# Layer 1 of a two-layer attention kernel: the two halves of the softmax sums merged by VectorE, the ones product in four column tiles of 256 columns

## The chip, the cores and the metric

The kernel runs on one core of a Trainium2 chip. The time is device microseconds of one execution; medians of several executions are given. In what follows, TensorE is PE in the profile, VectorE is DVE, ScalarE is ACT, PEld is TensorE's loading of weights, and the queue of SyncE, from which the transfers here are issued, is SPq.

## The reference, cut to what matters

Two attention layers over eight images of 64 channels and 64 x 64 positions, so 4096 queries and keys per image. Layer 0 has 8 channels in its scores; layer 1 normalises by groups, has 64 channels in its scores, and adds a projection.

```python
# layer 0
s = einsum('bci,bcj->bij', f, g); beta = softmax(s, axis=2)
o = einsum('bcj,bij->bci', hh, beta); x = x + o
# layer 1
attn = softmax(einsum('bqc,bkc->bqk', q, k) * scale, axis=-1)
out = einsum('bqk,bkc->bqc', attn, v)        # then a projection, + x
```

Each softmax needs the sum of the exponentials over all keys, one number per query. The change is about that sum in layer 1.

## The kernel before

A stage is one image in one layer. It has four chunks of 2 x 512 queries (h is the half of the queries), and a chunk has 16 steps of two key tiles (p = 0 and 1). In each step TensorE makes scores (s), ScalarE takes the exponential (e), TensorE weighs the values with it (acc, in PSUM), and VectorE adds e to a running sum (esum), 128 x 2048 elements. The stages follow in the order 0, 1, then alternating: layer 1 of image b-2 alternates with layer 0 of image b. During a layer-1 stage the next layer-0 image is prepared, at fixed steps.

When a chunk ends, this happens (cut; in order of the source):

```python
def finish(self, acc, esum, c, index):
    raw = work.tile([P, CW], F32, tag="raw", bufs=3, ...)
    self.total(raw, acc)              # copies the accumulator out of PSUM
    ...
    def sums(spare):                  # five steps later in layer 1
        for p in range(2):
            for h in range(2):        # ones product: sum over the 128 partitions
                matmul(z[ts(2*h+p, 32), :], ones, esum[:, p, h, :],
                       start=True, stop=True, tile_position=(0, 32*(2*h+p)))
        zs = work.tile([P, CW], F32, tag="zs", ...)
        nc.scalar.copy(zs, z)
        for h in range(2):
            for p in range(2):        # rows dealt over partitions by transfers
                row = 32 * (2*h + p)
                nc.sync.dma_start(zt[ts(h, C), p, :], zs[row : row+1, :])

    def reciprocals():
        nc.vector.tensor_add(zh, zt[:, 0, :], zt[:, 1, :])
        nc.vector.reciprocal(rt, zh)
        ...                           # to DRAM and back, spread over partitions
    def result():
        nc.vector.tensor_mul(raw, raw, r)
        self.residual(raw, c)

# layer 1
def total(self, raw, acc):
    nc.vector.tensor_copy(raw, acc[0])
    nc.vector.tensor_add(raw, acc[1], raw)

# layer 0, preparation of an image: steps of the stage in which it is done
return [(20, begin, True), (25, lambda: self.project(1), True)] + [...]
```

The accumulator of layer 1 has two banks, and those are all that its pool has; the next chunk's weighing can't start before `total` has copied them (in the trace of before, TensorE waits 0.88 us for that copy at 1258 us). VectorE works its queue in order: in that trace exponentials that ScalarE finished at 1223.59 and 1227.08 us are summed only from 1230.41 on, after VectorE had stood 7.61 us for the transfer of the sums. And `project` of the preparation issues 16 transfers of f and g rows from the same queue as the transfers of the sums.

## Time and profile before

| | before |
|---|---|
| time, median of 3 | 3190.0 us (3187.82 to 3190.19) |
| span of the profiled run | 3188.0 us |
| TensorE busy | 3116.8 us, 98% |
| VectorE busy | 2450.2 us, 77% |
| ScalarE busy | 2083.4 us, 65% |
| mean granted clock of TensorE | 0.996 |

The share of busy time says what an engine does over the whole span; the chain of waits (part 4 of the page) says whose work the end depended on. The lines of both are in the prediction.

### The profile page before, as it was taken

The numbers are of one execution on the slowest core, as the hardware profiler recorded it, in microseconds if no ns is written. First come the engines' busy times: TensorE is split into PE (matmuls) and PEld (weight loads), VectorE is DVE, ScalarE is ACT, GpSimd is POOL, SyncE is SP. The second block draws the span as 40 slices with busy tenths as digits, with TensorE's granted clock in tenths as the row PEclk, the third lists the DMA queues.
The fourth block names the chain that finished last, engine by engine and source line by source line (L and its number), as shares of the span: only waits on it lengthen the run. The fifth ranks groups of instructions, "written<-read, shape, count | busy, mean of one in ns | idle before, by whom it ended". The sixth has DMA issues, their size and how long they took to land.

```text
span 3188.0 us, 58576 instructions
## 1 busy us (share of the span) xinstructions
PE 3116.8 (98%) x25525; PEld 1106.0 (35%) x25525; DVE 2450.2 (77%) x1588; ACT 2083.4 (65%) x2257; POOL 16.7 (1%) x41
## 2 busy tenths in 40 slices
PE   7999999999999999999999999999999999999997
PEld 2333334333333334333333333333333333334432
DVE  6899766887678876788767887679866798666665
ACT  6787655776557765577655875558855587555554
POOL 2000000000000000000000000000000000000000
PEclk9999999999999999999999999999999999999999
DMA  3100010100101001010010100101001000000000
GB/s 69 34 8 17 11 34 8 28 21 8 35 8 28 21 8 34 8 28 21 8 34 8 31 19 7 38 5 35 18 5 41 2 21 18 5 21 15 9 14 15
DMA packets 66408, 63.54 MB, mean 20 GB/s; under 512 B 39408, under 2 KB 39488, under 8 KB 66144
## 3 DMA queue, kind: packets, MB, share of 16 engines
q1 hardware_dynamic: 65024, 59.56, 7.9%
q8 instruction: 202, 3.31, 0.4%
q14 instruction: 62, 0.51, 0.1%
q0 software_dynamic: 800, 0.15, 0.0%
q10 hardware_dynamic: 320, 0.01, 0.0%
HBM read 25.33 MB, written 8.65 MB: 11 GB/s over the span
## 4 chain that ended last, share of the span: by engine, by line
PE 87%; ACT 5%; DVE 4%; issue 2%; DMA 1%; SPq 0%; DVEq 0%; ACTq 0%
PE acc_l L122 51%; PE s_l L122 31%; ACT e_l L623 5%; DVE esum_l L595 3%; PE z_l L122 2%; PE qk_l L122 1%; PE v_l L122 1%; DMA r_l<-recips 0%; PE fg_l L122 0%; SPq L306 0%; DMA zt_l<-zs_l 0%; DVE split_l L371 0%; DVE vt_l L276 0%; DMA recips<-stash 0%; DMA x<-in_x_dram 0%
## 5 line engine op out<-in xcount | busy, mean ns | idle before, releaser
L623 ACT ACTIVATE e_l<-s_l 128x1024 f32<-128x1024 f32 x2048 | 1967.5, 1025 | 1062.0 <-PE s_l L122 1062.0
L595 DVE TENSOR_TENSOR esum_l<-esum_l,e_l 128x2048 f32<-128x2048 f32 x896 | 2050.6, 2289 | 390.1 <-ACT e_l L623 347.3
L122 PE MATMUL acc_l<-e_l,vt_l 64*64 64x512 f32 (+1 forms) x12288 | 1959.5, 595 | 6.7 <-DVE raw_l L524 5.9
L122 PE MATMUL s_l<-kq_l 64*64 64x512 f32 x8192 | 992.2, 589 | 1.5 <-DVE ve_l L443 1.5
L122 PEld LDWEIGHTS acc_l<-e_l,vt_l 64*64 64x64 f32 (+1 forms) x12288 | 594.2, 134 | 1067.2 <-issue 963.9
L122 PEld LDWEIGHTS s_l<-kq_l 64*64 64x64 f32 x8192 | 343.7, 133 | 543.0 <-issue 534.7
L122 PE MATMUL s_l<-fg_l 32*128 32x512 f32 x2048 | 272.0, 472 | 23.6 <-ACT e_l L623 15.5
L122 PEld LDWEIGHTS s_l<-fg_l 32*128 32x128 f32 x2048 | 108.0, 182 | 345.0 <-ACT e_l L623 213.2
L595 DVE TENSOR_TENSOR esum_l<-e_l,e_l 128x2048 f32<-128x2048 f32 x64 | 146.2, 2285 | 78.4 <-ACT e_l L623 78.4
L320 DVE TENSOR_TENSOR raw_l<-raw_l,r_l 128x512 f32<-128x512 f32 x64 | 44.0, 688 | 84.7 <-DMA r_l<-recips 84.7
L310 DVE TENSOR_TENSOR zh_l<-zt_l 128x8 f32<-128x8 f32 x64 | 10.5, 164 | 106.4 <-DMA zt_l<-zs_l 106.4
L122 PE MATMUL z_l<-esum_l,ones 128*32 128x512 f32 x512 | 68.4, 606 | 1.5 <-DVE vt_l L276 1.3
L524 DVE COPY raw_l<-acc_l 128x512 f32<-128x512 f32 x32 | 22.1, 690 | 41.5 <-PE acc_l L122 41.5
L302 ACT COPY zs_l<-z_l 128x512 f32<-128x512 f32 x64 | 38.2, 597 | 5.1 <-PE z_l L122 5.1
L498 ACT ACTIVATE kq_l<-qk_l,qkb 128x512 f32<-128x512 f32 x64 | 40.7, 697 | 0.0
L122 PE MATMUL qk_l<-xn_l,wqk 64*64 64x512 f32 x256 | 34.8, 611 | 0.0
L122 PE MATMUL v_l<-wvp,xn_l 64*64 64x64 f32 x1024 | 22.1, 223 | 8.4 <-ACT e_l L623 8.4
L122 PEld LDWEIGHTS v_l<-wh,x 64*64 64x64 f32 x1024 | 23.0, 136 | 15.9 <-issue 13.6
L122 PE MATMUL fg_l<-x,wfg 64*64 64x512 f32 x128 | 18.8, 652 | 9.7 <-DVE low L164 9.7
L122 PEld LDWEIGHTS v_l<-wvp,xn_l 64*64 64x64 f32 x1024 | 18.4, 134 | 18.6 <-ACT e_l L623 14.9
L525 DVE TENSOR_TENSOR raw_l<-acc_l,raw_l 128x512 f32<-128x512 f32 x32 | 22.1, 692 | 3.3
L528 DVE SCALAR_TENSOR_TENSOR raw_l<-raw_l,pb,x 128x512 f32<-128x512 f32 x32 | 24.0, 751 | 0.9
(81 smaller groups left out, 299.1 us busy)
## 6 DMA issues: line engine op xcount, KB each, us to landing
fg_l<-split_l SPq DMA_DIRECT2D x256, 64.0 KB, 2.0
r_l<-recips SPq DMA_DIRECT2D x128, 128.0 KB, 2.9
x<-in_x_dram SPq DMA_DIRECT2D x32, 256.0 KB, 4.8
kq_l<-kq_l SPq DMA_DIRECT2D x64, 128.0 KB, 2.3
out_dram<-raw_l SPq DMA_DIRECT2D x64, 128.0 KB, 2.3
zt_l<-zs_l SPq DMA_DIRECT2D x256, 2.0 KB, 1.8
recips<-stash SPq DMA_DIRECT2D x64, 4.0 KB, 1.4
wqk<-in_WqkvT_dram POOLq DMA_DIRECT2D x2, 32.0 KB, 5.3
```

Source lines behind the costliest of these rows:

```text
L122: in_order(nc.tensor.matmul(*args, **kwargs))
L302: nc.scalar.copy(zs, z)
L310: nc.vector.tensor_add(zh, zt[:, 0, :], zt[:, 1, :])
L320: nc.vector.tensor_mul(raw, raw, r)
L498: nc.scalar.activation(self.parts[:, h, cols], ps[:, h, :], AF.Identity, bias=k1["qkb"][:, h : h + 1],)
L524: nc.vector.tensor_copy(raw, acc[0])
L525: nc.vector.tensor_add(raw, acc[1], raw)
L528: nc.vector.scalar_tensor_tensor(o, o, k1["pb"], x_tiles[self.b][:, ts(c, CW)], op0=ALU.add, op1=ALU.add)
L595: nc.vector.tensor_add(esum, first if t == 1 else esum, e)
L623: nc.scalar.activation(e[:, p], ps, AF.Exp, scale=at.scale)
```

## The change

In layer 1, VectorE adds the two halves p of the running sum once per chunk (128 x 1024 elements). The ones product then has half as much to sum; its four column tiles take 256 columns each instead of 512. The intent is to take time off TensorE, which is busy 98%, at the cost of VectorE, which is busy 77%. The small sum after the transfers goes. Layer 0 only gets its four tiles in another order.

```diff
             self.total(raw, acc)
             zt = small.tile([P, 2, QP], F32, tag="zt", name=f"zt_{n}")
+            width = CW if self.kind == 0 else CW // 2
+            if self.kind == 1:
+                nc.vector.tensor_add(esum[:, 0], esum[:, 0], esum[:, 1])
 ...
-                for p in range(2):
-                    for h in range(2):
+                for h in range(2):
+                    for i in range(2):
+                        row = 32 * (2 * h + i)
+                        what = esum[:, i, h, :] if self.kind == 0 else esum[:, 0, h, ts(i, width)]
                         matmul(
-                            z[ts(2 * h + p, 32), :], ones, esum[:, p, h, :],
-                            start=True, stop=True, tile_position=(0, 32 * (2 * h + p)),
+                            z[row : row + 32, 0:width], ones, what,
+                            start=True, stop=True, tile_position=(0, row),
                         )
 ...
-                nc.vector.tensor_add(zh, zt[:, 0, :], zt[:, 1, :])
+                zh = zt[:, 0, :]
+                if self.kind == 0:
+                    nc.vector.tensor_add(zh, zh, zt[:, 1, :])
```

The cuts are the copy of z and the row transfers, which follow the new width.

More of the change, by code (lines that the diff above doesn't have):

```diff
@@ L294, in sums @@
                     z = ps_s.tile([P, 2, CW], F32, tag="s", name=f"z_{n}")[:, 0, :]
-                for p in range(2):
-                    for h in range(2):
+                zs = work.tile([P, CW], F32, tag="zs", name=f"zs_{n}")[:, 0:width]
+                for h in range(2):
+                    for i in range(2):
+                        row = 32 * (2 * h + i)
+                        what = esum[:, i, h, :] if self.kind == 0 else esum[:, 0, h, ts(i, width)]
                         matmul(
-                            z[ts(2 * h + p, 32), :], ones, esum[:, p, h, :],
-                            start=True, stop=True, tile_position=(0, 32 * (2 * h + p)),
-                        )
-                zs = work.tile([P, CW], F32, tag="zs", name=f"zs_{n}")
-                nc.scalar.copy(zs, z)
+                            z[row : row + 32, 0:width], ones, what,
+                            start=True, stop=True, tile_position=(0, row),
+                        )
+                nc.scalar.copy(zs, z[:, 0:width])
                 for h in range(2):
-                    for p in range(2):
-                        row = 32 * (2 * h + p)
-                        nc.sync.dma_start(zt[ts(h, C), p, :], zs[row : row + 1, :])
+                    for i in range(2):
+                        row = 32 * (2 * h + i)
+                        dst = zt[ts(h, C), i, :] if self.kind == 0 else zt[row : row + 32, 0, :]
+                        nc.sync.dma_start(dst, zs[row : row + 1, :])
             def reciprocals():
-                zh = small.tile([P, QP], F32, tag="zh", name=f"zh_{n}")
-                nc.vector.tensor_add(zh, zt[:, 0, :], zt[:, 1, :])
+                zh = zt[:, 0, :]
+                if self.kind == 0:
+                    nc.vector.tensor_add(zh, zh, zt[:, 1, :])
                 rt = stash[:, ts(index, QP)]
```

## The prediction

The length of the merge in it, 1.22 us, is an estimate; a straight line through two forms of the trace of before, 688 ns for a two-tensor operation of 512 columns (L320) and 2289 ns for one of 2048 (L595), gives 1222 ns at 1024. The four calls of one ones product are eight instructions in that trace, 512 for 64 products, which the prediction counts as two waves of four.

> **What bounds the kernel now.** I read the page first: busy shares, then the chain that ended last.
>
> ```profile
> PE 3116.8 (98%) x25525; PEld 1106.0 (35%) x25525; DVE 2450.2 (77%) x1588; ACT 2083.4 (65%) x2257; POOL 16.7 (1%) x41
> ...
> PE 87%; ACT 5%; DVE 4%; issue 2%; DMA 1%; SPq 0%; DVEq 0%; ACTq 0%
> ...
> L122 PE MATMUL z_l<-esum_l,ones 128*32 128x512 f32 x512 | 68.4, 606 | 1.5 <-DVE vt_l L276 1.3
> ```
>
> TensorE carries 87% of the chain; the ones product (z_l) is 68.4 us of its time, 64 products of eight instructions, so about 1.07 us each. Half of the 64 belong to layer 1, the only ones that get smaller: 34 us at stake, about 1% of 3190. The average hides where VectorE matters, though: it has 4% of the chain. So I went along the chain in order of time through one layer-1 stage (1141 to 1372 us). There a product looks like this:
>
> ```profile
> 1162.54 1.72 PE s_l L122 x16
> 1164.26 0.99 PE z_l L122 x8
> 1165.26 1.88 PE acc_l L122 x16
> ...
> 1278.61 0.46 PE v_l L122 x32
> ```
>
> Columns: start, length, what. TensorE runs without a gap from scores to product to weighing. Sixteen 512-column matmuls in 1.72 us are four waves of four concurrent tiles, 0.43 us a wave. Thirty-two 64-column matmuls (v_l) in 0.46 us are eight waves, 0.0575 us each. Between the two a column costs (0.43 - 0.0575) / 448 = 0.83 ns per wave, and a short wave is not held up by weight loads.
>
> Next, VectorE where one chunk of 512 queries ends and the next begins (VectorE's part of the timeline, with the idle time before an instruction in brackets):
>
> ```profile
> 1194.06 2.29 DVE L595 TENSOR_TENSOR esum_l<-esum_l,e_l 128x2048 f32<-128x2048 f32 x1 [0.44 <-ACT e_l L623]
> 1198.07 0.69 DVE L524 COPY raw_l<-acc_l 128x512 f32<-128x512 f32 x1 [1.71 <-PE acc_l L122]
> ...
> 1230.09 0.17 DVE L310 TENSOR_TENSOR zh_l<-zt_l 128x8 f32<-128x8 f32 x1 [7.61 <-DMA zt_l<-zs_l]
> ...
> 1243.59 14.26 DVE L595 TENSOR_TENSOR esum_l<-esum_l,e_l 128x2048 f32<-128x2048 f32 x6
> 1257.77 0.68 DVE L524 COPY raw_l<-acc_l 128x512 f32<-128x512 f32 x1
> 1258.56 0.69 DVE L525 TENSOR_TENSOR raw_l<-acc_l,raw_l 128x512 f32<-128x512 f32 x1
> ```
>
> The first boundary (chunk 0 to 1) has 1.71 us of idle time between the last sum and the copy of the accumulator: VectorE waits for TensorE. The second (chunk 1 to 2) has none. VectorE had stood 7.61 us for the sums' transfer, came late, and works back to back up to the copy. There TensorE waits for VectorE, because that copy frees an accumulator bank:
>
> ```profile
> 1257.85 0.61 DVE raw_l L524
> 1258.47 0.04 issue
> 1258.51 2.30 PE acc_l L122 x14
> ```
>
> The chain of waits passes from VectorE's copy to TensorE here, at 472, 865, 1258, 1651, 2044 and 2437 us: once in each layer-1 stage that also prepares a later layer-0 image, six times. I listed all 32 boundaries: 25 have 1.14 to 1.72 us of idle time before the copy, these six have none, and neither has the last one, at the end of the kernel:
>
> ```profile
> 3167.00 2.29 DVE L595 TENSOR_TENSOR esum_l<-esum_l,e_l 128x2048 f32<-128x2048 f32 x1 [1.14 <-ACT e_l L623]
> 3169.28 0.69 DVE L524 COPY raw_l<-acc_l 128x512 f32<-128x512 f32 x1
> 3169.44 1.06 PE L122 MATMUL z_l<-esum_l,ones 128*32 128x512 f32 x8 [0.18 <-PE acc_l L122]
> ```
>
> [...] 512 instructions of 606 ns mean make only 68.4 us busy, over four at a time; so halving the columns of all four tiles halves the streaming. [...] So the place of the merge in VectorE's queue decides its cost.
>
> **The change part by part.** The instruction order of the built kernel, which the diff does not tell, shows the 32 merges hoisted: directly after a chunk's last sum and *before* the accumulator copies, though the source has them after. Otherwise TensorE keeps its order and counts. The reordering of layer 0's four tiles (columns 0, 32, 64, 96) costs nothing I can find.
>
> *Product, layer 1.* Two waves [...] lose 256 columns each: 2 x 256 x 0.83 = 0.425 us; 0.99 us becomes about 0.57. The dearer restart after it (1.88 for 1.72) stays. Over 32: 13.6 us of TensorE time.
>
> *Merge.* 32 x 1.22 = 39 us more VectorE work. In 25 boundaries it falls into idle time before the copy (1.22 us in 1.59 to 1.72; at the one boundary with 1.14 us there is a second gap before it) and costs nothing. In the six late ones it moves the copy, and TensorE's restart, by its 1.22 plus the 0.10 us that dependent sums show between them: six of them take 14.26 us, 2.39 apart (6 x 2.29 = 13.74).
>
> *Small parts.* The zh sum of layer 1 goes: 0.164 us, with its gap 0.20, 32 times. The ScalarE copy of z has 256 columns; from 697 ns at 512 and 1120 at 1024 for the ACTIVATE forms, 0.83 ns a column, it falls from 0.597 to about 0.39 us. The row transfers stay four per chunk, half as long; I count nothing.
>
> *Sum.* (a) 25 products on an unbroken TensorE path: -25 x 0.425 = -10.6 us. (b) In the six stages, chunk 0's product (1214.42) lies inside the stretch in which the queue of transfers and then VectorE set when TensorE goes on at 1258: transfers of the split f and g rows are issued for 10.06 us before the sums' transfers and start at 1215.59, set by earlier VectorE work. Reaching that wait 0.425 us sooner buys nothing; the copy comes 1.32 - 0.20 = 1.12 us later: +6.7 us. (c) Tail: z waits for the merge, +1.32, then -0.425 (product), -0.21 (ScalarE copy), -0.20 (zh): +0.5 us. Together -10.6 + 6.7 + 0.5 = -3.4 us: 3186.6. I say 3187.
>
> **Rivals.** *TensorE decides alone:* all 32 savings arrive, 3176. For it: 98% busy, 87% of the chain. Against it: the six places where the chain passes through the copy with no slack before it. The form of this that I would believe is that the lighter transfers (half the rows per transfer) or their issue, 3 us for four in these stretches, shrink enough to give VectorE its 1.1 us back: 3180. *VectorE becomes the bound in layer 0:* there sums run nearly back to back (five in 11.87 us) and TensorE needs only 3.39 us for three blocks, 2.26 per sum of 2.37. Six layer-1 products run early in layer-0 stages; if VectorE takes back their 0.425 us, +2.6 us. If a merge also left VectorE late into layer 0, six times 1.2 more: 3197. Against it: before layer 0 the copy has 1.59 us idle before it and the next instruction another 1.84 for a transfer, so VectorE enters layer 0 no later. *A 256-column wave is not half as long* because weights or the switch of tiling limit it: with no saving, +7 us, 3197; the eight 64-column waves in 0.46 us speak against it.
>
> **Range and chances.** The terms are 10.6, 6.7 and 0.5 us, opposite in sign; each could be off by about a third, and layer 0 by 2.6. The runs before span 2.4 us. Range 3180 to 3194. Two per cent is 64 us, more than all the product and merge time together could move: faster 0.01, same 0.98, slower 0.01.
>
> **What would show it.** z_l with 256 columns at about 0.57 us a product (0.99 for layer 0); the new 128x1024 sum at 1.22 us, x32. In the six late boundaries, TensorE's wait for the copy of L524 (weight loads wait 1.6 to 2.3 us now) should grow by about 1.5 us each, 1.12 plus the 0.425 it arrives sooner; in the other boundaries the idle time before the copy should shrink to 0.4 or 0.5 us with no new wait. Stages of layer 1 with a late boundary should barely change (three products saved, 1.3 us, against 1.1 lost), and the last two layer-1 images should be 3.0 us shorter up to the tail. Wrong if the late boundaries lengthen by nothing, or if the idle time before the other copies is gone and TensorE waits there too.

## More of the kernel before

A single look (rounds 0) has the state "unknown" and is used for its trace, not for its time.

The granted clock is a part of the page that is easy to pass over: before, it is at full speed but for the beginning, one place at 126 us and the end.

## The result, and the profile after

| | before | after |
|---|---|---|
| time, median of 6 | 3189.54 us (3187.82 to 3190.85) | 3193.11 us (3189.17 to 3202.17) |
| span of the profiled run | 3188.0 us | 3196.6 us |
| mean granted clock, profiled run | 0.996 | 0.990 |
| sum of (1 - clock) x length | 13.6 us | 31.6 us |

The ratio is 1.0016, with a 95% interval from 1.0001 to 1.003. Ratios here are the mean time of one kernel's runs over that of the other's of the same rounds, so not quite the ratio of the medians. The change made the kernel slightly slower, and its runs spread over 13 us, where those of before spread over 3. A second set of five runs (e6 below) put it 10.0 us above before by the medians, with a ratio of 1.0021. The profiled run is the second slowest of its six, with a clock of 0.990; the two runs at the median have 0.993 and 0.992.

First the parts that did what they should. This is the page of the changed kernel, the parts that answer to those in the prediction:

```profile
PE 3118.1 (98%) x25525; PEld 1112.3 (35%) x25525; DVE 2483.8 (78%) x1588; ACT 2075.6 (65%) x2257; POOL 17.1 (1%) x41
...
PE 84%; DVE 6%; ACT 5%; issue 2%; DMA 1%; SPq 1%; ACTq 0%; DVEq 0%
...
L289 DVE TENSOR_TENSOR esum_l<-esum_l 128x1024 f32<-128x1024 f32 x32 | 39.2, 1225 | 1.1
```

Among the groups by form, the two widths of the product stand apart:

```profile
L122 PE MATMUL z_l<-esum_l,ones 128*32 128x512 f32 x256 | 34.7, 615 | 0.0
L122 PE MATMUL z_l<-esum_l,ones 128*32 128x256 f32 x256 | 20.4, 391 | 2.8 <-DVE esum_l L289 1.4 <-DVE vt_l L276 1.4
```

The narrow product has 20.4 us against 34.7 us for as many wide ones; the merge takes 1225 ns. Yet TensorE's busy time rose by 1.3 us, although its work fell by 14, and VectorE's share of the chain went from 4% to 6%. The place to look is the boundary of chunks 1 and 2, where the prediction had seen VectorE late. VectorE's timeline of the changed kernel there:

```profile
1246.71 14.27 DVE L603 TENSOR_TENSOR esum_l<-esum_l,e_l 128x2048 f32<-128x2048 f32 x6
1261.01 1.22 DVE L289 TENSOR_TENSOR esum_l<-esum_l 128x1024 f32<-128x1024 f32 x1
1262.16 0.68 DVE L532 COPY raw_l<-acc_l 128x512 f32<-128x512 f32 x1
```

The merge stands between the last sum and the copy, as the built order had it, with no idle time to fall into. TensorE's timeline, first before, then after, from the last scores ahead of its wait (columns: start, length, what, count; in brackets the idle time and what ended it):

```profile
1255.74 1.90 PE L122 MATMUL s_l<-kq_l 64*64 64x512 f32 x16
1258.51 2.30 PE L122 MATMUL acc_l<-e_l,vt_l 64*64 64x512 f32 x14 [0.88 <-DVE raw_l L524]
```

```profile
1258.72 1.90 PE L122 MATMUL s_l<-kq_l 64*64 64x512 f32 x16
1262.89 4.02 PE L122 MATMUL acc_l<-e_l,vt_l 64*64 64x512 f32 x16 [2.27 <-DVE raw_l L532]
1266.35 2.28 PE L122 MATMUL s_l<-kq_l 64*64 64x512 f32 x16
```

The wait grew from 0.88 to 2.27 us. But look at what comes after it: sixteen matmuls, which take 1.72 us from start to start in the unbroken stretches, take 3.46 us here (1262.89 to 1266.35). The same stretch cut into windows of 2 us shows why; the third number from the right is the granted clock:

```profile
1260.00:1262.00 2.00, 0.62 (x8) 0.00 (x0) 1.97 (x2) 1.77 (x2) 0.00 (x0) 1.00 0.00 0
1262.00:1264.00 2.00, 1.11 (x6) 0.60 (x10) 1.90 (x4) 0.00 (x0) 0.00 (x0) 0.73 0.00 0
1264.00:1266.00 2.00, 2.00 (x14) 0.61 (x10) 1.83 (x1) 0.00 (x0) 0.00 (x0) 0.50 0.00 0
1266.00:1268.00 2.00, 2.00 (x20) 0.67 (x16) 0.00 (x0) 0.16 (x1) 0.00 (x0) 0.92 0.00 0
```

After the wait the clock is halved for about 3.4 us (0.50 for 3.413 us by the clock's record), a loss of 1.70 us. In the run of before it stays at 1.00 through all six of these boundaries.

All six boundaries, with each ones product used as a milestone in both traces. "Copy later" is how much later the copy starts after the start of chunk 0's product; "step" is how much the time between chunk 0's and chunk 1's products grew:

| place (us, before) | TensorE's wait before | after | copy later | clock drop after it | step |
|---|---|---|---|---|---|
| 472 | 0.71 | 2.40 | +1.26 | yes | +2.48 |
| 865 | 1.02 | 2.77 | +1.33 | yes | +3.02 |
| 1258 | 0.88 | 2.27 | +0.98 | yes | +2.26 |
| 1651 | 0.88 | 2.11 | +0.80 | no | +0.80 |
| 2044 | 1.41 | 2.47 | +0.63 | yes | +2.18 |
| 2437 | 1.05 | 2.30 | +0.83 | yes | +2.50 |

At the one place where the clock did not drop, the step equals the lateness of the copy. Where it did, 1.2 to 1.7 us come on top. The sum of 13.24 us is 5.83 us of lateness and 7.41 us of drops.

Three more drops of this run stand inside layer-0 stages, at 1890, 2286 and 2682 us. There TensorE has no longer wait than before, only two gaps of 0.4 us for ScalarE, the same in both kernels. After those gaps (changed kernel, TensorE's timeline):

```profile
1889.69 0.50 PE L122 MATMUL s_l<-fg_l 32*128 32x512 f32 x2 [0.39 <-ACT e_l L631]
1890.61 0.52 PE L122 MATMUL s_l<-fg_l 32*128 32x512 f32 x2 [0.41 <-ACT e_l L631]
1891.06 4.42 PE L122 MATMUL acc_l<-e_l,vt_l 128*64 128x512 f32 x12
```

The same twelve matmuls before:

```profile
1887.04 2.79 PE L122 MATMUL acc_l<-e_l,vt_l 128*64 128x512 f32 x12
```

They take 4.42 us in place of 2.79. These three drops cost 5.0 us by the milestones.

The balance of the profiled runs, by milestones: 25 products -10.8, lateness at the six boundaries +5.8, drops after them +7.4, drops in layer 0 +5.0, the tail +0.6, the first stage, which has a drop of its own, +0.5. That is +8.6 us, the difference of the spans.

### The profile page after: what moved, and what is told of

Its sections match the earlier page's. It is cut to its first block, busy times and chain, and to the rows that moved or that the text cites. A ratio compares the mean times of both kernels' runs of the same rounds, so it can differ in the third digit from the quotient of the medians. Undisturbed runs are those within 1.5% of the kernel's fastest.

```text
span 3196.6 us, 58607 instructions
## 1 busy us (share of the span) xinstructions
PE 3118.1 (98%) x25525; PEld 1112.3 (35%) x25525; DVE 2483.8 (78%) x1588; ACT 2075.6 (65%) x2257; POOL 17.1 (1%) x41
## 4 chain that ended last, share of the span: by engine, by line
PE 84%; DVE 6%; ACT 5%; issue 2%; DMA 1%; SPq 1%; ACTq 0%; DVEq 0%
PE acc_l L122 50%; PE s_l L122 31%; DVE esum_l L603 5%; ACT e_l L631 5%; PE z_l L122 2%; PE qk_l L122 1%; PE v_l L122 1%; DMA r_l<-recips 1%; SPq L313 0%; PE fg_l L122 0%; DMA zt_l<-zs_l 0%; DMA recips<-stash 0%; DVE esum_l L289 0%; DVE split_l L379 0%; DVE vt_l L276 0%
## 5 line engine op out<-in xcount | busy, mean ns | idle before, releaser
L603 DVE TENSOR_TENSOR esum_l<-esum_l,e_l 128x2048 f32<-128x2048 f32 x896 | 2051.3, 2289 | 401.8 <-ACT e_l L631 358.5
L320 DVE RECIPROCAL stash<-zt_l 128x8 f32<-128x8 f32 x64 | 12.9, 202 | 90.7 <-DMA zt_l<-zs_l 89.9
L122 PE MATMUL z_l<-esum_l,ones 128*32 128x512 f32 (+1 forms) x512 | 55.2, 503 | 2.8 <-DVE esum_l L289 1.4
L289 DVE TENSOR_TENSOR esum_l<-esum_l 128x1024 f32<-128x1024 f32 x32 | 39.2, 1225 | 1.1
L308 ACT COPY zs_l<-z_l 128x512 f32<-128x512 f32 (+1 forms) x64 | 31.6, 493 | 5.0 <-PE z_l L122 5.0
```

The source lines that it names most:

```text
L122: in_order(nc.tensor.matmul(*args, **kwargs))
L289: nc.vector.tensor_add(esum[:, 0], esum[:, 0], esum[:, 1])
L308: nc.scalar.copy(zs, z[:, 0:width])
L603: nc.vector.tensor_add(esum, first if t == 1 else esum, e)
```

## The experiments

The theory after this look (A): the merge, standing before the copy, lengthens TensorE's wait at the six late boundaries; after such a wait the granted clock is halved for about 3.4 us. The rivals: VectorE's added work as such (B), drops caused by the shorter product (C), drops as luck of the run (D).

| run | edit | this, median | before, median | ratio (95% interval) |
|---|---|---|---|---|
| e1_merge_only | merge alone | 3205.91 | 3189.57 | 1.0049 (1.0035 to 1.0063) |
| e2_product_only | product alone | 3177.90 | 3189.57 | 0.9962 (0.9948 to 0.9975) |
| e3_merge_behind | merge behind the copies | 3181.26 | 3189.57 | 0.9971 (0.9958 to 0.9985) |
| e4_after_later_prep | changed, later preparation | 3167.30 | 3189.57 | 0.9928 (0.9914 to 0.9941) |
| e5_before_later_prep | before, later preparation | 3180.08 | 3189.21 | 0.9965 (0.9952 to 0.9979) |
| e6_after_again | changed kernel again | 3199.24 | 3189.21 | 1.0021 (1.0008 to 1.0035) |
| e7_merge_512 | smaller merge alone | 3200.53 | 3189.21 | 1.0027 (1.0013 to 1.0041) |
| e8_busy_wait | wait filled with matmuls | 3191.43 | 3190.93 | 1.0002 (0.9988 to 1.0015) |
| e9_look_1, e9_look_2 | changed kernel, one look each | 3198.44, 3196.49 | | |

All but e2 give the correct result.

### The merge alone

```diff
 # in the kernel before
             self.total(raw, acc)
+            if self.kind == 1:
+                junk = work.tile([P, 2, CW], F32, tag="junk", bufs=1, name=f"junk_{n}")
+                nc.vector.tensor_add(junk, esum[:, 0], esum[:, 1])
```

> The kernel before, with the 128x1024 sum of layer 1 added at the same place of VectorE's queue but into a scratch tile, so that the product stays at 512 columns. Theory A (the merge holds back the accumulator copy at the six late boundaries, TensorE's wait there grows to over 2 us, and after such a wait the granted clock is halved for about 3.4 us): the six waits of TensorE go from 0.7-1.4 us to 2.0-2.7 us, four to six of them are followed by a stretch at clock 0.50, and the time is 6 x 1.3 us + about 5 x 1.3 us = 10 to 17 us above before. Theory C (clock drops come from the shorter product, which makes TensorE's activity lighter): waits grow alike, no clock drop beside those of before, +7 to +9 us. Theory B (38 us more work of VectorE slow the kernel wherever they stand): lags also grow at the other 26 boundaries.

It cost 16.3 us by the medians. The six waits are 1.75 to 2.64 us, and five of them are followed by a drop. At the boundary shown above (TensorE's timeline and the clock, two views):

```profile
1263.46 3.12 PE L122 MATMUL acc_l<-e_l,vt_l 64*64 64x512 f32 x14 [1.98 <-DVE raw_l L527]
```

```profile
1266.00:1268.00 2.00, 2.00 (x12) 0.71 (x8) 0.40 (x1) 0.00 (x0) 0.00 (x0) 0.50 0.00 0
```

The time between products grew by 1.53 to 3.33 us at the six boundaries and by less than 0.3 us at every other product of a chunk, apart from a shift at the start. So the added work costs nothing where VectorE has idle time: B falls. The wide product has the drops too: C falls. The layer-0 stages had no extra drop in this run.

### The product alone

```diff
 # in the changed kernel; layer 1's sums are wrong on purpose
-            if self.kind == 1:
-                nc.vector.tensor_add(esum[:, 0], esum[:, 0], esum[:, 1])
```

> The changed kernel without the merge: wrong sums in layer 1 on purpose (half of the keys are left out), everything else the same. Theory A: 25 products outside the late stretches give 0.425 us each, the tail 0.8 us, the six late waits grow only by the 0.4 us that TensorE comes sooner (to 1.1-1.8 us), no clock drop after them: 10 to 13 us below before. Theory C (drops from the shorter product): drops stay as in the changed kernel, 0 to 5 us below before. Theory D (the drops are luck of the run): drops at places that do not repeat.

The result is wrong (relative error 0.15). It gains 11.7 us by the medians, about what the prediction had worked out for the products and their part of the tail (10.6 + 0.8). The waits at the six places are 1.20 to 1.55 us. One drop did follow, after the longest of them, and one stood in a layer-0 stage.

### The merge behind the copies, at the six late boundaries only

```diff
-            self.total(raw, acc)
+            last = self.total(raw, acc)
 ...
-                nc.vector.tensor_add(esum[:, 0], esum[:, 0], esum[:, 1])
+                merged = nc.vector.tensor_add(esum[:, 0], esum[:, 0], esum[:, 1])
+            if self.kind == 1 and c == 1 and self.b < B - 2:
+                tc.add_manual_dep(merged.ins, last.ins.name, ..., reason="order")
 ...
-            nc.vector.tensor_add(raw, acc[1], raw)
+            return nc.vector.tensor_add(raw, acc[1], raw)
```

> The changed kernel with the merge of chunk 1 put behind the two accumulator copies in VectorE's queue, in the six layer-1 images with a late boundary; the other 26 merges stay. Theory A: the six waits of TensorE are 1.1-1.8 us, no clock drop after them, 9 to 12 us below before, and within 2 us of the product alone. Theory B: VectorE has the same work, so the time stays at that of the changed kernel, 0 to 8 us above before.

The same instructions, six of them standing two places later in VectorE's queue: 8.3 us below before by the medians, where the changed kernel is 3.6 and, in e6, 10.0 above. VectorE's timeline at the boundary that was shown above:

```profile
1255.22 0.68 DVE L539 COPY raw_l<-acc_l 128x512 f32<-128x512 f32 x1
1256.01 0.69 DVE L540 TENSOR_TENSOR raw_l<-acc_l,raw_l 128x512 f32<-128x512 f32 x1
1256.62 1.22 DVE L289 TENSOR_TENSOR esum_l<-esum_l 128x1024 f32<-128x1024 f32 x1
```

TensorE waits 1.21 to 1.74 us at the six places, and no drop follows any of them. By the means of the runs this is 2.4 us slower than the product alone, slightly more than I had expected; the expectation of 9 to 12 us below before was missed by under 1 us.

### The changed kernel with a later preparation of the next image

```diff
-            return [(20, begin, True), (25, lambda: self.project(1), True)] + [
+            first, second = (20, 25) if self.b < 2 else (27, 31)
+            return [(first, begin, True), (second, lambda: self.project(1), True)] + [
```

> The changed kernel with the preparation of the next layer-0 image moved from steps 20 and 25 of the layer-1 stage to 27 and 31, so that the 16 transfers of f and g no longer stand in the queue ahead of the transfers of chunk 0's sums. If the late boundary comes from that queue (VectorE stands 7.6 us for the sums' transfer), VectorE's wait falls to about 2.3 us, the copies have idle time before them at all boundaries, TensorE's six waits vanish: 13.6 us of products + 6 us of waits = 16 to 21 us below before. If VectorE is late for another reason, the waits stay and the time is that of the changed kernel.

The result is correct and is the fastest: 22.3 us below before, all five runs between 3166.76 and 3167.73, and a little better than the 16 to 21 us expected. VectorE's timeline at the sums of chunk 0 and at the boundary that used to be late:

```profile
1211.45 0.20 DVE L320 RECIPROCAL stash<-zt_l 128x8 f32<-128x8 f32 x1 [1.67 <-DMA zt_l<-zs_l]
...
1246.23 1.22 DVE L289 TENSOR_TENSOR esum_l<-esum_l 128x1024 f32<-128x1024 f32 x1
...
1248.56 0.68 DVE L533 COPY raw_l<-acc_l 128x512 f32<-128x512 f32 x1
```

The wait for the sums' transfer is 1.67 us in place of 7.61, because the transfers of f and g no longer stand before it in the queue. TensorE has no wait of over 0.6 us at any of the six places. The copy has no idle time before it, contrary to the expectation, but it comes early enough for TensorE: the merge is still before it and now costs no wait. VectorE's own work for the preparation (the split of f and g, 2 us each time) is still ahead of the boundary, from 1231.04 and 1245.63 us on, so that work alone does not make the copy late. What made it late was the order of the transfers in the queue: in the trace of before, the 16 transfers of f and g took 10.06 us to issue from one queue, 0.63 us each where one lands in 2.0 us (median), and VectorE stood 7.61 us for rows that were issued after them.

### The kernel before with the later preparation

The edit is that of the last experiment, in the kernel before.

> The kernel before with only the later preparation (steps 27 and 31), no merge, 512-column product. Splits the gain of e4: if the schedule is worth the six waits alone (0.7-1.4 us each), 5 to 8 us below before, and the change is then worth 12 to 14 us on top of it (3167 against about 3180), all of its product saving. If instead the two parts are not additive (the merge or the short product still cost something in e4), the schedule alone gives 10 us or more.

It gains 9.1 us by the medians, between the two expectations. The waits removed add up to 5.95 us (0.71 + 1.02 + 0.88 + 0.88 + 1.41 + 1.05). Part of the other 3 us is the restart after a wait: at 1258, fourteen matmuls take 1.77 us from start to start where sixteen take 1.72 in unbroken stretches, because the second bank is copied only from 1258.56 on. The rest was not followed. The change on top of this schedule is worth 12.8 us (3180.08 against 3167.30, on two chips), which is within what all its products should save.

### The changed kernel again, and two more looks

> The changed kernel once more, on this chip, with its profile. Theory A: the six waits of 2.1-2.8 us come again at the same places; clock drops follow most of them. The drops inside layer-0 stages (three in the first profile, at places without a longer wait) need not repeat (theory D for those alone): if they come again at the same places they belong to the change, if not they are luck of the run. Time 0 to 13 us above before, following the granted clock of the run.

> The changed kernel, one more profile: which of the six waits of 2.1-2.8 us are followed by a clock drop, and whether the six places inside layer-0 stages (two gaps of 0.4 us each, no longer wait than before) drop all, some or none. By theory D they vary from run to run.

> As e9_look_1, a third and last further profile of the changed kernel.

The four profiles of the changed kernel have 24 waits at the six places, 2.09 to 3.25 us long. 20 were followed by a drop. In the profile of e6 all six were, and there were six more drops, one in each layer-0 stage from 710 to 2690 us; that execution took 3206.25 us. The two looks had two such layer-0 drops and none. So the drops after the waits belong to the change, and those in layer 0 vary from run to run (what sets them is worked out further down). This is most of the changed kernel's spread. In both timed sets the slowest run has the lowest clock (0.989 and 0.988), the fastest the highest (0.994 and 0.993).

### A smaller merge

```diff
 # as the merge alone, but 512 columns
+                nc.vector.tensor_add(junk[:, 0, 0:512], esum[:, 0, 0, 0:512], esum[:, 1, 0, 0:512])
```

> As e1, with the scratch sum of only 512 columns (0.69 us instead of 1.22). Theory A: the six waits are 1.5-2.2 us, +0.8 us each = 5 us from the waits; clock drops after some of them only (none up to about 1.5 us, all above about 2.3 us so far), 5 to 10 us above before.

The waits are 1.58 to 2.23 us. The four above 2 us were followed by a drop, those of 1.58 and 1.75 were not, and one drop stood in layer 0. It cost 11.3 us by the medians, a little over the expectation: more of the waits than I thought were long enough.

### The wait filled with matmuls

```diff
 # in the changed kernel, main loop
                 at.scores(ps, t, p, c)
+                if at.kind == 1 and c == 2 and at.b < B - 2 and t == 1:
+                    at.scores(ps, t, p, c)
```

> The changed kernel with 16 score matmuls (1.72 us) of chunk 2 issued twice, the same values into the same bank, just before TensorE's late wait, in the six layer-1 images: TensorE is busy during what was its wait, and the accumulator copy comes as late as before. If the granted clock drops because TensorE stood idle there (theory A), TensorE's idle time at the six places falls to 0.4-1.1 us, no clock drop follows, and the time is 6 to 8 us (five or six drops at about 1.3 us) below the changed kernel of the same rounds or runs, about 3186 to 3190, although TensorE has 10 us more work. If the drops have another cause, they stay, and the time is that of the changed kernel or above.

This is the direct test that idleness of TensorE brings the drop. The copy comes at least as late as in the changed kernel (44.25 to 45.85 us after chunk 0's product, against 44.23 to 44.89); TensorE issues the same scores twice instead of standing. Its timeline and the clock at the boundary shown above (two views of this kernel):

```profile
1255.44 2.33 PE L122 MATMUL s_l<-kq_l 64*64 64x512 f32 x20
1258.18 2.30 PE L122 MATMUL acc_l<-e_l,vt_l 64*64 64x512 f32 x14 [0.41 <-DVE raw_l L532]
```

```profile
1258.00:1260.00 2.00, 1.82 (x16) 0.76 (x20) 1.90 (x3) 0.86 (x1) 0.00 (x0) 1.00 0.00 0
```

Five of the six waits are 0.41 to 1.43 us and have no drop; the sixth was still 2.01 us, longer than expected, and has one. One more stood in layer 0. With 10 us of useless work more, the kernel took 3191.43 us, slightly more than the 3186 to 3190 expected and 0.5 us above before, against 3198.44 and 3196.49 us for the changed kernel's single looks, and 3193.11 and 3199.24 us in its two timed sets.

## Why the prediction was wrong, point by point

The forecast was 3 us faster; the kernel became 3.6 us slower by the medians, and 10.0 when it was run again (e6), within 2% as forecast.

- *What bounds the kernel.* Right: TensorE nearly everywhere, VectorE at six boundaries. e3 and e4 show that these six decide the change's worth.
- *Product, 0.425 us each.* Right. 0.99 became 0.57 us; the milestones give 10.8 us for the 25 products, with 10.6 forecast, and e2 gains 11.7. The last two layer-1 images became 3.1 us shorter up to the tail, with 3.0 forecast.
- *The other 25 merges at boundaries with idle time.* Right in that they cost nothing: in e1 no product's milestone shifts there. In the changed kernel 19 of these copies keep 0.45 us of idle time, as forecast; the six before a layer-0 stage have none left, but TensorE does not wait there.
- *Chunk 0's product in the six stages buys nothing.* Right: the stretch from it to the first transfer of f and g is 1.23 to 1.24 us in both kernels, and the rest follows from there.
- *Copy 1.12 us later at the six boundaries.* About right. From the multiplication by the reciprocals to the copy it is 22.10 us before and 23.36 after, +1.26; ahead of that 0.29 was gained on average (from 0.07 lost to 0.63 gained), where the forecast counts 0.20 for the missing small sum alone. Net +0.97 us, 5.8 us over the six where the forecast had 6.7.
- *Tail, +0.5.* Right: the merge put the product 1.26 us later, and from the product to the end it went 0.63 us faster: +0.6.
- *"Together -10.6 + 6.7 + 0.5 = -3.4 us".* **This step failed.** The sum priced TensorE's wait by its own length alone. I had forecast that wait correctly ("about 1.5 us" more; it was 1.40 more on average) and did not ask what it does to the work after it. The missing term is the granted clock: a drop costs 1.70 us of the clock, net 1.2 to 1.7 us (probably because TensorE then waits less for the second bank; not shown). In the profiled run five drops after the waits made 7.4 us and three in layer 0 made 5.0; the terms that the forecast did have measure -10.8 + 5.8 + 0.6 = -4.4 us there. e8 shows the cause: fill the wait and the drops at the six places are gone but for one, after the 2.01 us that were left there. The page's row PEclk shows only nines in both kernels; it was too coarse to warn.
- *Rivals.* None of them had this. "VectorE becomes the bound in layer 0" did not come: layer 0 has no wait for VectorE, and e4 keeps all 13 us.

Why a wait of 3.25 us can pass without a drop while one of 1.55 us brings one, and why layer 0 had up to six drops in one run and none in another, can largely be read from the traces. Within each of the twelve traces all drops begin a whole number of steps of 3.4133 us apart, to within about 1 ns, so these steps can be laid as windows over the whole trace; a drop begins where a window ends. The table counts TensorE's idle time by window: the 60 late waits (ten profiles), and layer 0's two gaps of 0.4 us, which come once in each of the seven layer-0 stages after the first, in each of the twelve. Its limits are read off afterwards and were not forecast, and the ends of matmuls, from which idle time is counted, are modelled.

| what falls into one window | times followed by a drop |
|---|---|
| a late wait, at most 1.43 us of it in one window | 0 of 24 |
| a late wait, 1.55 to 2.01 us of it in one window | 7 of 12 |
| a late wait, over 2.01 us of it in one window | 24 of 24 |
| layer 0's two gaps, the first beginning 1.53 to 1.81 us after the window's start | 15 of 15 |
| layer 0's two gaps at any other point of the window | 0 of 69 |

By the length of the whole wait, the same 60 do not part cleanly: none of 20 below 1.5 us was followed by a drop, 3 of 7 between 1.5 and 2 us, 28 of 33 above 2 us. They part better by how much of a wait falls into one window: 0 of 24, 7 of 12 and 24 of 24. The end of a window cut the wait of 3.25 us in e9_look_1, which had no drop, into 1.70 and 1.55 us, and the one of 2.11 us at 1651 into 1.04 and 1.08. So theory D is only half right: the drops in layer 0 vary, but not at random; they go by where the gaps meet the window. The four traces of the changed kernel had 11 in 28 such stages, the other eight 4 in 56. In e6 the drops repeat every 396 us, which is 116 of these steps, so each period met the window at the same point. No run shifted that point on purpose; the runs differ in it by themselves. What stays open is why 1.55 to 2.01 us sometimes suffice and sometimes not, and why layer 0's gaps count in that part of the window alone.

## What to carry to other kernels

Work moved to an engine "with slack" costs what it costs at the places where that engine is late; list all the places, and look at the built order, because a merge before a copy and a merge behind it differ by 12 to 18 us here (3.6 and 10.0 us above before in two sets, against 8.3 below). A wait of the matmul engine had a second price here: from about 1.5 us within one window on, the clock after it could be halved for 3.4 us (1.70 us lost), so read the granted clock in short windows behind every wait that a change lengthens. And ask why the engine is late: the cure was not in the merge but in the order of the transfer queue, and it turned a loss of 4 to 10 us into a gain of 22.
